# A graph layer with gathers of h held longer, lists of rows and the second dst moved between them, and one-hot rows in buffers of their own

## The chip, the cores and the metric

The kernel runs on one core of a Trainium2 chip. The metric is the time of one execution in microseconds on the device: the median of several runs. A profile of one execution shows what each engine did: PE (TensorE, products), DVE (VectorE), ACT (ScalarE), POOL (GpSimd, which here issues the indexed gathers) and SP (SyncE, which issues plain transfers).

## The reference

One message-passing layer over 6,250 nodes and 206,250 edges that are sorted by their target (`dst`).

```python
h = jnp.maximum(_layernorm(x, axis=-1), 0.0)
msg = h[src] + edge_attr_64                       # 206250 x 64
agg = jax.ops.segment_sum(msg, dst, num_segments=6250)
out = x + jax.nn.relu(agg @ W1 + b1) @ W2 + b2
```

All arrays are float32; x is 6250 x 64, W1 64 x 128 and W2 128 x 64.

## The kernel before

The sum over edges is split. The edges' own features are summed by target with one-hot products: `chunk_hot` (L380) makes one-hot rows on DVE, `chunk_sum` (L392) multiplies them with the features into the PSUM tile `bank`, ACT copies the result (`by_node`, L395) and `chunk_place` (L404) adds it to a block's PSUM tile `pv`. The part `h[src]` is not gathered for most edges. The kernel counts instead how often each source stands at each target: for lists of 128 edges, `count` makes one-hot rows of the source's low and high parts (`hot_lo`, `hot_key`, L699), multiplies them (L707, PSUM tile `pc`), ACT copies the counts to SBUF (L709), and `multiply` multiplies the counts with h (L742 and L745, into `pv`).

The last 24 groups of 1,024 edges (GA to G) go another way. `load_h` (L823) loads a group's features into a tile `pfeat` (four buffers), and POOL adds the rows of h to them with 8 indexed gathers per group from a table in memory (L252). `features_h` takes a pair of groups: `sum_groups` makes one-hot rows `hotp` (L421), multiplies them with the two tiles (L425, also into `bank`), and copies to `sum_p` (L428); `add_sums` (L414) adds that to the sums on DVE. At its end `features_h` asks for the pair two further on (`fetch_h`), whose tiles take the two buffers that have just been read.

The main loop has 310 steps: 22 blocks of targets with 14 steps each, one of them with 16. A pair of one-hot tiles is made on DVE in every even step, for two steps. Work that does not belong to the counting is hung on steps: `before` runs ahead of a step's counting, `later` behind its products. POOL's order is settled when the kernel is built: `queue` holds gathers with a planned cost each, `pool[0]` is POOL's planned time, `clock(n)` the planned time of step n (1.6 us per step for the first 14, then 1.38), and after each step POOL gets what is planned to begin up to 5 us later. A pair is multiplied in the first step for which

```python
if h_next < G and fetched.get(h_next + 1, 1e9) + LAND_US <= clock(n):
    features_h(h_next)
    h_next += GB
    add_later(n + 5)
```

where `fetched` is the planned time at which the pair's last gather was issued. What has not been multiplied by the end of the loop is multiplied behind it.

The head, before the loop, does three things. It finds where each list of edges begins: `fetch_row` gathers rows of `dst` (15 lists of 128), `seek` counts in them on ACT (L268), and `place` (L272, L274) writes `first` and `first_i` on DVE. From `first_i`, `fetch_pair` gathers the packed words of two lists, `unpack_pair` and `turn_pair` make the keys. It normalizes x: `norm_mean`, `norm_center` (which lets ACT square), `norm_var`, `norm_root`, `norm_scale`, `norm_h` (which writes the table); `norm_b` and `norm_c` split h in three bfloat16 parts within the first steps. And it finds the targets of the edge chunks: `chunk_starts`, `chunk_rows`, `chunk_columns`, `chunk_index` give `cols_i`, `fetch_dst` gathers `dstq`, `chunk_nodes` (L337, L338) and `chunk_turn` (L345) turn it into `rel`, which `chunk_hot` reads.

The order of each engine is that of the program text: a manual schedule records the operations as they are called. An engine that waits holds all that stands behind it in its queue.

Of the kernel before, what the change touches and what calls it, by code (L numbers as in the profile page):

```python
# [18 lines left out]
P = 128  # L19
N = 6250  # L20
E = 206250
D = 64
# [11 lines left out]
J = 8  # L34
# [3 lines left out]
W = 42  # L38
# [56 lines left out]


HEAD_US = 1.6
STEP_US = 1.38
GATHER_US = 2.2
WORDS_US = 2.6  # L100
LAND_US = 5.0
NEED_P = N - 31 * GP - 6


@with_exitstack
def gnn_kernel(ctx: ExitStack, tc: tile.TileContext, x, src_t, dst_t, dst_g, edge, w1, b1, w2, b2, out):
# [196 lines left out]
    def chunk_columns(t0, t1, tag="po", bufs=1):  # L303

        px = ps.tile([P, NT + 1], F32, tag=tag, name="pcols", bufs=bufs)
        n = (t1 - t0) * RC
        assert n <= JP * RC
        quarters = late.tile([P, JP * RC, JQ], F32, tag="dstq", bufs=2, name="quarters")[0:1, :n]
        nc.vector.tensor_tensor(quarters, starts[:, t0 * RC:t1 * RC].unsqueeze(2).to_broadcast([1, n, JQ]),
                                row_e.unsqueeze(1).to_broadcast([1, n, JQ]), op=OP.add)  # L310
        rows = [(t, quarters[:, (t - t0) * RC:(t - t0 + 1) * RC, :]) for t in range(t0, t1)]
        if t0 == 0:
            rows.append((NT, row_n))
        for t, of in rows:
            nc.tensor.matmul(px[:, t:t + 1], of.rearrange("o c q -> o (c q)"), ones[0:1, 0:1], start=True, stop=True)
        known["t", t0] = px
# [12 lines left out]
    def fetch_dst(t):  # L329
        dsts[t] = late.tile([P, CQ], I32, tag="dstq", bufs=2, name="dstq")  # L330
        gather(dsts[t], dst_g.rearrange("q h (k o) -> (q h k) o", o=1), cols_i[:, t:t + 1])
# [85 lines left out]
    def sum_groups(g, tiles):  # L417
        pa = bank[:, :GB * W].rearrange("p (b w) -> p b w", b=GB)
        for b in range(GB):
            hot = work.tile([P, J, W], F32, tag="hot", name="hotp")  # L420
            nc.vector.tensor_tensor(hot, rel_p[:, g - GA + b, :].unsqueeze(2).to_broadcast([P, J, W]),  # L421
                                    iota[:, :W].unsqueeze(1).to_broadcast([P, J, W]), op=OP.is_equal)
            for j in range(J):
                k = j % 2 * D
                nc.tensor.matmul(pa[k:k + D, b, :], tiles[b][:, j, :], hot[:, j, :],  # L425
                                 start=(j < 2), stop=(j >= J - 2))
        sum_p = work.tile([P, GB, W], F32, name="sum_p", bufs=1)
        nc.scalar.activation(sum_p, pa, AF.Copy)  # L428
        to_add.append((g, sum_p))
# [122 lines left out]
    nc.scalar.dma_start(packed.rearrange("(q k) o -> q (k o)", q=QA), dstn[:QA].rearrange("q h k -> q (h k)"))  # L552
    seek(0, 6)
    place(0, 3)
    norm_mean()
    place(3, 3)
    fetch_pair(0)
    for i in range(6, 11):
        fetch_row(i)
    for k in range(3):  # L560
        norm_center(k)
        seek(6 + k, 1)
    fetch_pair(2)
    for k in range(3):
        norm_var(k)
    norm_root()
# [287 lines left out]
    for g in range(GA, GA + 2):  # L854
        load_h(g)
    for i in range(11, IC):
        fetch_row(i)
    place(6, 3)
    chunk_starts(0, 2 * RC, "pc", 2)
# [5 lines left out]
    turn_pair(0)  # L865
    seek(9, 3)
    norm_scale()
    chunk_index(0, 2)
    fetch_dst(0)
    fetch_dst(1)  # L870
    for k in range(3):
# [5 lines left out]
    todo = {}  # L877

    def then(k, f):
        todo[k] = f()  # L880

    before = {
        1: [lambda: seek(12, 3), lambda: chunk_nodes(0)],
        2: [lambda: [fetch_h(g) for g in range(GA, GA + 4)], lambda: chunk_turn(0)],
        3: [lambda: place(9, 3), lambda: open_pv(0, True)],
        5: [lambda: place(12, 3)],
        7: [lambda: norm_b(0)],
        9: [lambda: norm_b(1)],
        11: [lambda: norm_b(2)],
        13: [find_groups],  # L890
        15: [lambda: norm_c(0), lambda: clear(0, 5)],
        17: [lambda: norm_c(1), lambda: clear(1, 5)],
        19: [lambda: norm_c(2), lambda: clear(2, 5)],
        21: [lambda: clear(3, 5)],
        23: [lambda: clear(4, 5)],
# [18 lines left out]
    for k in range(1, (IC + 1) // 2):  # L914
        n = 12 + 10 * k
        if k > 1:
            before.setdefault(max(n - 20, 3), []).append(lambda k=k: queue.insert(0, (WORDS_US, lambda: fetch_pair(2 * k))))
        before.setdefault(n, []).append(lambda k=k: unpack_pair(2 * k))
        before.setdefault(n + 1, []).append(lambda k=k: turn_pair(2 * k))
    for t in range(1, NT):  # L920
        n = 24 if t == 1 else 64 + 4 * t
        if t > 1:
            before.setdefault(n, []).append(lambda t=t: queue.insert(0, (GATHER_US, lambda: fetch_dst(t))))
        before.setdefault(n + 8, []).append(lambda t=t: chunk_nodes(t))
        before.setdefault(n + 9, []).append(lambda t=t: chunk_turn(t))
# [57 lines left out]
    for n, (b, s) in enumerate(steps):  # L983
# [23 lines left out]
        if n >= 3:  # L1007
            if h_next < G and fetched.get(h_next + 1, 1e9) + LAND_US <= clock(n):
                features_h(h_next)
                h_next += GB  # L1010
                add_later(n + 5)
# [152 lines left out]
```

## Time and profile before

| | |
|---|---|
| median of 9 runs | 539.95 us (538.48 to 542.29) |
| the profiled execution | 539.93 us, span 538.2 us |
| PE busy | 456.3 us (85%) |
| DVE busy | 417.1 us (77%) |
| POOL busy | 424.1 us (79%) |
| ACT busy | 353.3 us (66%) |
| main loop, first one-hot rows to last counting products | 40.5 to 513.5 us of the span |
| the 192 gathers of h | 46.3 to 508.0 us, 1.9 us each |

A line of the timeline gives start, duration, engine, line, operation, tiles and count; in brackets stands how long the engine had rested before and what it waited for. A line of the windows gives the window, its length, the busy time of PE, weight loads, DVE, ACT and POOL, the granted TensorE clock (1.00 is full), the share of the DMA engines and GB/s. In the chain, the shares say on which engine's work the end of the run hung.

### The profile page before, as it was taken

The numbers are of one execution on the slowest core, as the hardware profiler recorded it, in microseconds if no ns is written. First come the engines' busy times: TensorE is split into PE (matmuls) and PEld (weight loads), VectorE is DVE, ScalarE is ACT, GpSimd is POOL, SyncE is SP. The second block draws the span as 40 slices with busy tenths as digits, with TensorE's granted clock in tenths as the row PEclk, the third lists the DMA queues.
The fourth block names the chain that finished last, engine by engine and source line by source line (L and its number), as shares of the span: only waits on it lengthen the run. The fifth ranks groups of instructions, "written<-read, shape, count | busy, mean of one in ns | idle before, by whom it ended". The sixth has DMA issues, their size and how long they took to land.

```text
span 538.2 us, 19106 instructions
## 1 busy us (share of the span) xinstructions
PE 456.3 (85%) x8183; PEld 384.8 (71%) x8184; DVE 417.1 (77%) x618; ACT 353.3 (66%) x534; POOL 424.1 (79%) x265
## 2 busy tenths in 40 slices
PE   3015678899987999888989999999999999999994
PEld 3014566777876887667778877888888778888883
DVE  4787998778797979849789769788697597797720
ACT  4357897677574756787657765767667676677621
POOL 6676898888897878889888888888888888888600
PEclk9999899999998999999999999999999999999998
DMA  8839703555655666554575665665666666667540
GB/s 225 227 117 285 191 12 65 141 139 144 168 141 157 159 160 174 144 119 130 135 176 130 142 149 120 144 175 144 143 175 142 146 172 147 171 144 146 132 130 15
DMA packets 113544, 79.04 MB, mean 147 GB/s; under 512 B 32920, under 2 KB 108686, under 8 KB 113230
## 3 DMA queue, kind: packets, MB, share of 16 engines
q1 hardware_dynamic: 83962, 65.99, 42.1%
q0 software_dynamic: 29200, 10.25, 16.1%
q10 hardware_dynamic: 292, 1.52, 0.9%
q8 instruction: 66, 1.08, 0.8%
q14 instruction: 24, 0.20, 0.1%
HBM read 73.74 MB, written 3.99 MB: 144 GB/s over the span
## 4 chain that ended last, share of the span: by engine, by line
PE 69%; DVE 12%; ACT 6%; issue 5%; DMA 5%; POOL 2%; DVEq 0%; ACTq 0%
PE pc L707 22%; PE pv L742 16%; PE pv L745 11%; PE bank L392 10%; DVE hot_lo L699 4%; ACT counts L709 3%; DVE hot_key L699 3%; PE pv L404 3%; PE ph L798 2%; DMA dstq<-in_dst_g,cols_i 2%; PE po L805 2%; POOL rows L252 2%; DMA rows<-in_dst_g,row_i 2%; PE bank L425 2%; ACT over L666 1%
## 5 line engine op out<-in xcount | busy, mean ns | idle before, releaser
L252 POOL DMA_INDIRECT pfeat<-table,src_p x192 | 363.9, 1895 | 62.1 <-issue 53.3
L709 ACT ACTIVATE counts<-pc 128x882 bf16<-128x882 f32 x310 | 272.9, 909 | 42.9 <-PE pc L707 29.7
L707 PE MATMUL pc<-hot_key,hot_lo 128*128 128x147 bf16 x1860 | 175.1, 231 | 30.4 <-DVE hot_key L699 15.3
L699 DVE TENSOR_TENSOR hot_lo<-iota_lo,keys 128x1536 bf16<-128x1536 bf16 x155 | 147.7, 953 | 41.0 <-PE pc L707 38.7
L707 PEld LDWEIGHTS <-hot_lo 128*128 128x128 bf16 x1860 | 134.9, 100 | 59.5 <-issue 25.3
L699 DVE TENSOR_TENSOR hot_key<-iota_key,keys 128x1776 bf16<-128x1776 bf16 x155 | 166.9, 1077 | 0.0
L742 PE MATMUL pv<-counts,h 128*128 128x252 bf16 (+1 forms) x1078 | 148.7, 272 | 0.1
L742 PEld LDWEIGHTS <-h 128*128 128x128 bf16 x1078 | 99.0, 97 | 8.2 <-issue 0.2
L745 PE MATMUL pv<-counts,h 128*64 128x252 bf16 (+1 forms) x1078 | 76.0, 275 | 0.0
L395 ACT ACTIVATE by_node<-bank 128x128 f32<-128x128 f32 x66 | 18.4, 279 | 84.1 <-PE bank L392 49.0
L392 PE MATMUL bank<-feat,hot 128*21 128x64 f32 x3168 | 66.5, 222 | 6.4 <-issue 3.8
L392 PEld LDWEIGHTS bank<-feat,hot 128*21 128x21 f32 x3168 | 49.4, 101 | 21.5 <-issue 17.5
L745 PEld LDWEIGHTS <-h 128*64 128x64 bf16 x1078 | 54.2, 111 | 3.6 <-issue 0.4
L380 DVE TENSOR_TENSOR hot<-rel,iota 128x504 f32<-128x504 bf16 x66 | 44.6, 677 | 8.8 <-PE bank L425 8.4
L252 POOL DMA_INDIRECT words<-packed,first_i x15 | 25.8, 1720 | 8.0 <-DMA packed<-dstn 3.7
L421 DVE TENSOR_TENSOR hotp<-dst_p,iota 128x336 f32<-128x336 f32 x24 | 11.9, 506 | 25.1 <-PE bank L392 18.5
L252 POOL DMA_INDIRECT rows<-in_dst_g,row_i x15 | 17.0, 1132 | 6.7 <-issue 3.4
L404 PE MATMUL pv<-select,by_node 128*64 128x42 f32 x264 | 21.4, 244 | 0.7 <-ACT by_node L395 0.7
L404 PEld LDWEIGHTS pv<-select,by_node 128*64 128x64 f32 x264 | 13.4, 137 | 9.4 <-issue 1.1
L294 PE MATMUL pstart<-begins,first 128*1 128x9 f32 (+2 forms) x30 | 1.3, 172 | 19.8 <-DVE first L272 19.4
L798 PE MATMUL ph<-sums,w1s 128*128 128x252 f32 (+1 forms) x50 | 15.5, 391 | 1.5 <-DVE sums L414 0.9
L754 DVE TENSOR_TENSOR sums<-sums,pv 128x252 f32<-128x252 f32 x22 | 9.0, 409 | 8.6 <-PE pv L745 8.6
(171 smaller groups left out, 274.7 us busy)
## 6 DMA issues: line engine op xcount, KB each, us to landing
feat<-in_edge SPq DMA_DIRECT2D x132, 384.0 KB
pfeat<-in_edge SPq DMA_DIRECT2D x24, 256.0 KB
pfeat<-table,src_p POOLq DMA_INDIRECT x192
out_y<-y SPq DMA_DIRECT2D x24, 63.0 KB
xs<-in_x SPq DMA_DIRECT2D x4, 315.0 KB
dstn<-in_dst_g SPq DMA_DIRECT2D x1, 1024.0 KB
table<-xl SPq DMA_DIRECT2D x2, 512.0 KB
packed<-dstn ACTq DMA_DIRECT2D x1, 768.0 KB
```

The lines of the kernel that those rows point to most:

```text
L252: nc.gpsimd.indirect_dma_start(out=rows, out_offset=None, in_=source, in_offset=bass.IndirectOffsetOnAxis(ap=index, axis=0), compute_op=op)
L380: nc.vector.tensor_tensor(hot_of[u][:, :n].rearrange("p c j w -> p (c j) w"), rel[:, c:c + n].rearrange("p c q k -> p (c q k)").unsqueeze( ...
L392: nc.tensor.matmul(bank[q * QP:q * QP + WQ, i * D:(i + 1) * D], hot[:, i, j, :], feat[i][:, j, :], start=(k == 0), stop=(k == JP - 1))
L395: nc.scalar.activation(by_node[u][:, :n].rearrange("p c d -> p (c d)"), bank[:, :n * D], AF.Copy)
L404: nc.tensor.matmul(pvs[b][0][i * D:(i + 1) * D, a:a + CN], of[:, i, :], select, start=False, stop=False)
L421: nc.vector.tensor_tensor(hot, rel_p[:, g - GA + b, :].unsqueeze(2).to_broadcast([P, J, W]), iota[:, :W].unsqueeze(1).to_broadcast([P, J, ...
L699: nc.vector.tensor_tensor(hot.rearrange("p t (m o) -> p t m o", o=2), iota_k.rearrange("p (m o) -> p m o", o=2).unsqueeze(1).to_broadcast( ...
L707: nc.tensor.matmul(pc[:, k, m * K:(m + 1) * K], hot_lo[:, j, :], hot_key[:, j, :K], start=True, stop=True)
L709: nc.scalar.activation(counts[b % 2][:, :, s * ST * V:(s + 1) * ST * V].rearrange("p h (k m) -> p h k m", k=2), pc[:, :, :ST // 2 * K].rea ...
L742: nc.tensor.matmul(pv, h3[:, h, :2 * D], of, start=(h == 0 and not clear), stop=False)
L745: nc.tensor.matmul(pv[k:k + D, :], h3[:, h, 2 * D:], of, start=False, stop=(h >= HI - 2))
L798: nc.tensor.matmul(ph[:, :n], w1s, agg[:, start[b]:start[b + 1]], start=True, stop=True)
```

## The change

- `sum_groups` makes its one-hot rows in blocks of four columns of edges (128 x 168) in a tag `hotp` of its own with two buffers, four blocks per pair of groups. Before, a block held eight columns (128 x 336) and shared the two buffers of the tag `hot` with `chunk_hot`.
- The tiles `quarters` and `dstq` share one buffer instead of two.
- A pair of groups is multiplied once its last gather was planned 22 us ago (`HELD_US`), no longer 5 (`LAND_US`).
- In the head, seven lists' rows are fetched instead of fifteen; `norm_mean` comes ahead of the first `place`, and the squares come ahead of the `seek` of lists 3 to 6. Rows 7 to 10 and 11 to 14 are put at the front of POOL's queue at steps 3 and 14, and their `seek` and `place` go to steps 12 to 14 and 20 to 22.
- The third pair of word gathers is issued in the head, behind the first dst. The dst gathers of 1 to 4 are queued at step 24 and at 74, 84, 94 (before: in the head, and at 72, 76, 80); each is used 8 steps later as before.

```diff
+HELD_US = 22.0
...
-        quarters = late.tile([P, JP * RC, JQ], F32, tag="dstq", bufs=2, name="quarters")[0:1, :n]
+        quarters = late.tile([P, JP * RC, JQ], F32, tag="dstq", name="quarters")[0:1, :n]
...
-        dsts[t] = late.tile([P, CQ], I32, tag="dstq", bufs=2, name="dstq")
+        dsts[t] = late.tile([P, CQ], I32, tag="dstq", name="dstq")
...
         for b in range(GB):
-            hot = work.tile([P, J, W], F32, tag="hot", name="hotp")
-            nc.vector.tensor_tensor(hot, rel_p[:, g - GA + b, :].unsqueeze(2).to_broadcast([P, J, W]),
-                                    iota[:, :W].unsqueeze(1).to_broadcast([P, J, W]), op=OP.is_equal)
             for j in range(J):
-                k = j % 2 * D
-                nc.tensor.matmul(pa[k:k + D, b, :], tiles[b][:, j, :], hot[:, j, :],
-                                 start=(j < 2), stop=(j >= J - 2))
+                k = j % 4
+                if k == 0:
+                    hot = work.tile([P, 4, W], F32, name="hotp")
+                    nc.vector.tensor_tensor(hot, rel_p[:, g - GA + b, j:j + 4].unsqueeze(2).to_broadcast([P, 4, W]),
+                                            iota[:, :W].unsqueeze(1).to_broadcast([P, 4, W]), op=OP.is_equal)
+                h = slice(j % 2 * D, (j % 2 + 1) * D)
+                nc.tensor.matmul(pa[h, b, :], tiles[b][:, j, :], hot[:, k, :], start=(j < 2), stop=(j >= J - 2))
...
-    seek(0, 6)
+    seek(0, 3)
+    fetch_row(6)
+    norm_mean()
     place(0, 3)
-    norm_mean()
-    place(3, 3)
     fetch_pair(0)
-    for i in range(6, 11):
-        fetch_row(i)
     for k in range(3):
         norm_center(k)
-        seek(6 + k, 1)
+        if k < 2:
+            seek(3 + 2 * k, 2)
+    norm_var(0)
+    norm_var(1)
+    place(3, 4)
     fetch_pair(2)
-    for k in range(3):
-        norm_var(k)
+    norm_var(2)
     norm_root()
...
-    for i in range(11, IC):
-        fetch_row(i)
-    place(6, 3)
...
-    seek(9, 3)
     norm_scale()
     chunk_index(0, 2)
     fetch_dst(0)
-    fetch_dst(1)
+    fetch_pair(4)
...
+    def rows_later(a, z):
+        queue[:0] = [(1.25, lambda i=i: fetch_row(i)) for i in range(a, z)]
...
-        1: [lambda: seek(12, 3), lambda: chunk_nodes(0)],
+        1: [lambda: chunk_nodes(0)],
...
-        3: [lambda: place(9, 3), lambda: open_pv(0, True)],
-        5: [lambda: place(12, 3)],
+        3: [lambda: open_pv(0, True), lambda: rows_later(7, 11)],
+        12: [lambda: seek(7, 2)],
+        13: [lambda: seek(9, 2), find_groups],
+        14: [lambda: place(7, 4), lambda: rows_later(11, IC)],
...
+        20: [lambda: seek(11, 2)],
+        21: [lambda: clear(3, 5), lambda: seek(13, 2)],
+        22: [lambda: place(11, 4)],
...
-        if k > 1:
-            before.setdefault(max(n - 20, 3), []).append(lambda k=k: queue.insert(0, (WORDS_US, lambda: fetch_pair(2 * k))))
+        if k > 2:
+            before.setdefault(n - 20, []).append(lambda k=k: queue.insert(0, (WORDS_US, lambda: fetch_pair(2 * k))))
...
-        n = 24 if t == 1 else 64 + 4 * t
-        if t > 1:
+        n = 24 if t == 1 else 54 + 10 * t
+        if t > 0:
             before.setdefault(n, []).append(lambda t=t: queue.insert(0, (GATHER_US, lambda: fetch_dst(t))))
...
-            if h_next < G and fetched.get(h_next + 1, 1e9) + LAND_US <= clock(n):
+            if h_next < G and fetched.get(h_next + 1, 1e9) + HELD_US <= clock(n):
```

More of the change, by code (lines that the diff above doesn't have):

```diff
@@ L889, in gnn_kernel @@
         11: [lambda: norm_b(2)],
-        13: [find_groups],
         15: [lambda: norm_c(0), lambda: clear(0, 5)],
@@ L893, in gnn_kernel @@
         19: [lambda: norm_c(2), lambda: clear(2, 5)],
-        21: [lambda: clear(3, 5)],
+        20: [lambda: seek(11, 2)],
+        21: [lambda: clear(3, 5), lambda: seek(13, 2)],
+        22: [lambda: place(11, 4)],
         23: [lambda: clear(4, 5)],
```

## The prediction

> **What bounds the kernel now.** I read the page's busy shares and chain first, then the rests of each engine, then the timeline at the head, at a group of gathers late in the loop, and at the end.
>
> ```profile
> PE 456.3 (85%) x8183; PEld 384.8 (71%) x8184; DVE 417.1 (77%) x618; ACT 353.3 (66%) x534; POOL 424.1 (79%) x265
> PE 69%; DVE 12%; ACT 6%; issue 5%; DMA 5%; POOL 2%; DVEq 0%; ACTq 0%
> L252 POOL DMA_INDIRECT pfeat<-table,src_p x192 | 363.9, 1895 | 62.1 <-issue 53.3
> ```
>
> PE carries the chain, so after the head the loop runs at PE's pace. POOL's 79% hides a second bound: the 192 gathers of h follow one another without a pause from 46 us on (363.9 us busy, 53.3 us of issue gaps), and nothing in the chain shows it because POOL is done at 508 us while the last of its groups is read at 524 us. The end of the loop shows how near that is:
>
> ```profile
> 466.37 1.13 PE L425 MATMUL bank<-hotp,pfeat 128*64 128x42 f32 x32
> 467.10 1.78 SPq L823 DMA_DIRECT2D pfeat<-in_edge  x2
> 472.14 2.06 POOL L252 DMA_INDIRECT pfeat<-table,src_p  x1 [1.14 <-PE bank L392]
> 502.63 1.55 POOL L252 DMA_INDIRECT pfeat<-table,src_p  x1 [0.30 <-issue]
> 504.48 1.65 POOL L252 DMA_INDIRECT pfeat<-table,src_p  x1 [0.30 <-issue]
> 506.44 1.56 POOL L252 DMA_INDIRECT pfeat<-table,src_p  x1 [0.30 <-issue]
> 494.25 0.96 PE L707 MATMUL pc<-hot_key,hot_lo 128*128 128x147 bf16 x12
> 523.94 1.13 PE L425 MATMUL bank<-hotp,pfeat 128*64 128x42 f32 x32
> ```
>
> The tenth pair of groups is multiplied at 466.37; that frees two pfeat buffers, SP loads the last pair's edge rows into them, and POOL, which had to wait 1.14 us, starts the last 16 gathers 5.8 us after the products began. The last one starts at 506.44. So the place of the tenth pair in the loop fixes when the last gather can land.
>
> The head, and a long gather in it:
>
> ```profile
> 18.56 3.42 DVE L449 TENSOR_REDUCE stat<-xl 128x49 f32<-128x3136 f32 x1
> 32.26 0.19 DVE L465 TENSOR_SCALAR stat<-stat 128x49 f32<-128x49 f32 x1
> 36.82 0.16 DVE L320 CAST cols_i<-pcols 128x2 int32<-128x2 f32 x1 [0.26 <-PE pcols L315]
> 39.37 2.03 POOL L252 DMA_INDIRECT dstq<-in_dst_g,cols_i  x1 [0.31 <-issue]
> 45.35 0.42 DVE L337 TENSOR_SCALAR dstq<-dstq,cols 128x384 f32<-128x384 int32 x1 [2.91 <-DMA dstq<-in_dst_g,cols_i]
> 65.26 10.83 POOL L252 DMA_INDIRECT words<-packed,first_i  x1 [0.30 <-issue]
> 166.43 0.42 DVE L337 TENSOR_SCALAR dstq<-dstq,cols 128x384 f32<-128x384 int32 x1 [3.35 <-DMA dstq<-in_dst_g,cols_i]
> 170.00:173.00 3.00, 3.00 (x24) 2.48 (x24) 2.90 (x6) 2.04 (x3) 1.14 (x1) 0.50 0.14 16
> ```
>
> DVE sums x, the variance is scaled at 32.26, the columns for dst are known at 36.82, but POOL issues dst 0 only at 39.37, behind lists of rows; DVE stands 2.91 us for it. Again at 166.43 DVE stands 3.35 us for dst 2; PE then rests 2.59 us, and the last line shows the granted clock at 0.50 for the three microseconds behind that rest.
>
> **The head: -5.8 us.** The mean moves ahead of the first lists and ACT's squares ahead of seeks 3 to 6. DVE is free from 15.6; x has landed by 18.56 at the latest. With the rows' durations (mean 3.42 + 0.34, centre 1.14, square 1.06, two seeks 1.2, variance 1.2) the scaling falls at 28.1 if the mean starts at 15.6 and at 30.6 if it starts at 18.56; I take the middle, 29.3, 3.0 earlier than now. The chain to cols_i loses 0.27 us of list arithmetic: 33.55. On POOL, seven rows and four word gathers are over by 27.3 (each 0.95 + 0.3, packed landing at 21.4 as now), so dst 0 is issued at once and used 5.98 us later, as now: 39.5 instead of 45.35. The gain is 5.8 us (4.5 to 7.0 from the two ends). The second dst, two words and the rows' lists queue behind dst 0 while POOL waits for the table anyhow (3.03 us of rest now), so they cost nothing there; without that cover they cost 4 x 1.25 us. The table, and gathers of h with it, come 3.0 us earlier; four rows and dst 1 in between (6.5 us) take that back, less a word pair moved ahead (2.6): POOL gains nothing. DVE is busy without a gap from 53 to 76 us, so the 5.8 us survive to step 22.
>
> **The held groups: the end.** HELD_US makes a pair wait 22 us of planned time instead of 5. Placing the pairs by the planner's rule, products stand after steps 33, 65, 97, 123, 149, 174, 200, 225, 251, 276, 302 and once after the loop before; after the change at 55, 86, 116, 143, 168, 194, 219, 245, 270, 296 and twice after the loop. The tenth pair, which lets the last 16 gathers begin, is now at step 296. That step's PE work ends at 494.7 in the trace. With G the time saved by then, the sum is:
> - start of the tenth pair's products: 494.7 - G
> - to the first of the last 16 gathers: +5.8 (466.37 to 472.14)
> - 15 intervals: 13 us of loop remain, 6 intervals at 2.29 (472.14 to 506.44), then 9 at 1.9 (last two rows, DVE mostly idle): +30.8; the last one's own 1.6
> - landing: the 16th gather ended at 95.64 and its products ended at 98.44 without a rest, so at most 2.6; a dst gather landed 4.5 after its end. I take 2.5 (0 to 4.5)
> - last product 0.1 and the unchanged end: 538.2 - 525.1 = +13.1
> - PE's clock: it would reach these products at 523.9 - G and stand some 10 us; after 2.59 us of rest it got 0.50 for about 3.5 us, so half of that is lost: +1.7 (0 to 1.7)
>
> That is a span of 550.3 - G, and with 1.7 us around the span (539.93 - 538.2) a time of 552.0 - G. The profiled 539.93 equals the median 539.95. The change gains only if G passes 12.
>
> **G after the head.** dst gathers move to 54 + 10t, use eight steps later. Before dst 2, POOL now has 37 gathers of h instead of 40, nine words instead of eleven, but four rows and dst 1 more: 2.9 us less, and it starts 3.0 earlier, so it is issued near 155 and lands near 160.5; step 82 wants it near 165.8 - 5.8 = 160. The rest of 2.59 us and the slow clock behind it (half of 3.5) go but for a little: -3.5 (0 to -4.3). The tile is single now, so the next dst gather waits for the transposes of the last; those come one step after its use and the gathers 12 us apart, so I cost that at nothing; if late, it holds POOL for 2.1 us, as one did at 171.9.
>
> One-hot rows: DVE makes four blocks of 168 instead of two of 336. A block is between 0.25 (half of 506 ns) and 0.51; 0.30 by the 128x252 rows at 0.41: 0.2 us more DVE per pair, hidden where DVE leads. Two waits go: "hotp <- PE bank L392" 18.5 us over 7 and "hot <- PE bank L425" 8.4 over 4. One comes: the third block takes the first one's buffer, so DVE stands until PE has done the first four products of this very pair. Behind it DVE has block four, then hot_lo and hot_key of the next two steps, for which PE waits. If the pair ends an odd step, PE has nothing else: 0.2 + 2 x 0.30 + 0.87 + 1.0 = 2.7, less the 0.85 left of the pair's products: 1.8 us. If it ends an even step, one step of work covers it but for 0.4. Before step 296 four are odd (55, 143, 219, 245) and five even: 9.2 us. Rests of PE around products now, from PE's timeline: 0.46, 0.97, 0.43, 0.43, 0.91, 0.49, 0.43, 0.91, in sum 5.0; and one pair fewer stands before step 296 (1.13). Net +3.1; the ends are -6 (all rests go, nothing comes) and +8.
>
> G = 5.8 + 3.5 - 3.1 = 6.2, so 545.8 us.
>
> **A rule weighed.** Rows 11 to 14 are now gathered near 62 to 67, and ACT wants them at steps 20 and 21, near 69, with DVE and PE behind. In that stretch one gather took 10.83 us now, with DVE running two-input instructions without a gap from 65 to 75, while the three gathers ahead of it (59.70 to 64.95) took 1.55 beside the same kind of instruction. One in ten gathers between 46 and 76 was caught, so I leave it out of the sum and price it as a rival. The Trainium skill, "SBUF — State Buffer", section "Who interferes with whom", says that a DVE instruction with two SBUF inputs contends with a GpSimd instruction that reads SBUF; if the gather's index counts as such a read, all four rows would be held until DVE itself stops, and the estimate would be 553; the short gathers speak against so strict a reading.
>
> **The rivals.**
> - Lockout: the long gather of 65.26 falls on the lists of rows. DVE goes gap-free to about 69, rows follow to 74, land by 79, and DVE, waiting in place, loses about 7.5 us: 553. For it: the 10.83. Against it: nine in ten gathers passed.
> - Faster, by DVE's freedom: the 26.9 us of DVE rests on products go and take PE's rests on hot_key with them (15.3 us in the list of waits), because DVE stands in the third block only where it has a lead. It decides once G passes 13.7. With the head at 7.0, dst at 4.3 and +6 from the buffers, G is 17.3 and the time 535. Against it: the wait in the third block is certain in the order of DVE.
> - No difference: G between 10.4 and 13.7; or G between 5.8 and 9.1 with all gathers 1.86 apart and no slow clock (2.9 and 1.7 us less), so that the end eats the head's gain almost exactly: 540. Against the second: 2.29 beside a working DVE.
> - That holding the pairs does nothing, because gathers lie off the path: then 552.0 is replaced by 539.9 and the time is 534. It falls with the 1.14 us rest of POOL at 472.14: POOL already follows the products.
>
> **How the numbers follow.** Slower by the late last gathers, 541.6 to 549.5: 0.57. Lockout or worse, above that: 0.14. Faster (both ways): 0.14. Within 0.3% (1.6 us, about what a measurement here can tell from no change): 0.15. The range 538.5 to 551 leaves out most of the faster case and the upper half of the lockout.
>
> **What would show it.** Right: dst 0 used near 39.5; the tenth pair's products near 488; POOL resting before the last 16 gathers and the last starting near 525; PE resting some 10 us on pfeat near 518 to 529, then a granted clock of 0.50. Wrong: POOL done before PE leaves the loop; PE's rests on hot_key after products gone; a row gather of 5 us or more near 65.

## The result and the profile after

The changed kernel takes 560.12 us (median of 20 runs, 554.75 to 563.6) against 540.25 for the kernel before in the same comparison (62 runs): a ratio of 1.0358, 95% interval 1.0336 to 1.0379. The forecast was 545.8 with a range up to 551. The sign was right, the size was missed by 14 us. The profiled execution has a span of 558.1 us. Two of the 20 runs, and below two of the four of c_hotp4_held5 and one of the four of a_hotp4_held5, are more than 1.5% above the fastest of their kernel; no difference is read from these alone.

The rows of its page that correspond to those shown of the kernel before, the busy shares and the gathers of h:

```profile
PE 470.1 (84%) x8183; PEld 393.5 (71%) x8184; DVE 418.8 (75%) x640; ACT 356.0 (64%) x534; POOL 411.0 (74%) x265
L254 POOL DMA_INDIRECT pfeat<-table,src_p x192 | 359.7, 1873 | 88.0 <-issue 53.0
```

Of its timeline, the tenth pair with the last 16 gathers, the head, and dst 2 (start, duration, what; the rest before it in brackets):

```profile
503.32 0.67 PE L429 MATMUL bank<-hotp,pfeat 128*64 128x42 f32 x16
504.05 1.34 SPq L827 DMA_DIRECT2D pfeat<-in_edge  x2
508.14 2.00 POOL L254 DMA_INDIRECT pfeat<-table,src_p  x1 [5.36 <-PE pc L711]
538.35 1.54 POOL L254 DMA_INDIRECT pfeat<-table,src_p  x1 [0.30 <-issue]
542.09 0.44 PE L429 MATMUL bank<-hotp,pfeat 128*64 128x42 f32 x2 [1.49 <-DMA pfeat<-table,src_p]
...
28.49 0.19 DVE L468 TENSOR_SCALAR stat<-stat 128x49 f32<-128x49 f32 x1
32.75 0.16 DVE L322 CAST cols_i<-pcols 128x2 int32<-128x2 f32 x1 [0.27 <-PE pcols L317]
38.93 0.44 DVE L339 TENSOR_SCALAR dstq<-dstq,cols 128x384 f32<-128x384 int32 x1 [0.56 <-DMA dstq<-in_dst_g,cols_i]
169.33 0.41 DVE L339 TENSOR_SCALAR dstq<-dstq,cols 128x384 f32<-128x384 int32 x1
```

The head and the end came as forecast. dst 0 is used at 38.93 (forecast 39.5), dst 2 without a rest. From the tenth pair's products at 503.32 to the end of the span it is 54.8 us (forecast 55.6). What failed lies between. The products should have begun at 488.5, six us earlier than the work of that step before; they began at 503.32. The list of waits shows where to look (total in us, number of waits, longest). First the kernel before, then the changed one:

```profile
DVE hotp L421 <- PE bank L392: 18.5, 7, 5.4
PE pc L707 <- DVE hot_key L699: 15.3, 16, 2.6
POOL pfeat L252 <- PE pc L707: 2.7, 9, 0.3
```

```profile
DVE hotp L426 <- PE bank L429: 41.4, 17, 6.1
PE pc L711 <- DVE hot_key L703: 27.2, 15, 5.6
POOL pfeat L254 <- PE pc L711: 27.1, 8, 7.1
```

DVE stands 41.4 us ahead of one-hot rows, where it stood 18.5 before; PE's rests on hot_key rose from 15.3 to 27.2; and POOL, which hardly waited for PE in its line of gathers before (2.7), waits 27.1.

To see where time goes I took the start of ACT's eviction of the counts (L713) at each of the 310 steps and set it against the kernel before. The head's lead is 6.8 us at step 12. By step 32 it has become a loss of 2.2. Between steps 55 and 60, at the first pair of groups, another 4.7 us are lost, of which 1.1 are the pair's own products. Between steps 75 and 85, where dst 2 fell, 3.5 us come back. The loop then wavers between a lead of 0.6 and a loss of 3.6 up to step 180, loses 4 us at each of the pairs of steps 219 and 245, and ends at a loss of 9.3 (step 309: 522.8 against 513.5). The pair at step 55 shows the new wait in the timeline:

```profile
127.42 0.57 DVE L426 TENSOR_TENSOR hotp<-dst_p,iota 128x168 f32<-128x168 f32 x2
133.09 0.58 DVE L426 TENSOR_TENSOR hotp<-dst_p,iota 128x168 f32<-128x168 f32 x2 [5.10 <-PE bank L429]
133.59 0.96 DVE L703 TENSOR_TENSOR hot_lo<-iota_lo,keys 128x1536 bf16<-128x1536 bf16 x1
134.47 1.08 DVE L703 TENSOR_TENSOR hot_key<-iota_key,keys 128x1776 bf16<-128x1776 bf16 x1
...
132.05 0.62 PE L429 MATMUL bank<-hotp,pfeat 128*64 128x42 f32 x16
133.48 0.68 PE L429 MATMUL bank<-hotp,pfeat 128*64 128x42 f32 x16 [0.81 <-DVE hotp L426]
135.60 1.66 PE L711 MATMUL pc<-hot_key,hot_lo 128*128 128x147 bf16 x12 [1.45 <-DVE hot_key L703]
```

And the windows of the same stretch (time, length, then busy time of each engine, granted clock, DMA share, GB/s):

```profile
134.00:137.00 3.00, 1.55 (x18) 1.43 (x15) 3.00 (x4) 0.68 (x2) 0.00 (x0) 0.75 0.70 191
137.00:140.00 3.00, 3.00 (x26) 2.49 (x23) 2.98 (x5) 2.07 (x3) 2.67 (x2) 0.68 0.14 16
```

DVE makes two half blocks at 127.42 and is then some four us ahead of PE. The third needs the first one's buffer, so DVE stands 5.10 us until PE gets there, and arrives with no lead at all: PE waits 0.81 in the pair and 1.45 behind it, and its granted clock (third number from the end) falls to 0.75 and 0.68. The forecast had priced the bubble, the work that PE must wait for (1.8 us for pairs in odd steps, 0.4 for even ones). Step 55 is odd; the bubble here is 2.3, a slow clock comes on top, and DVE has its lead to earn again. The clock is the smaller part: of the ten pairs in the loop three are followed by 3.41 us at a clock of 0.50 (from 135.5, 388.1 and 429.0), which loses at most 1.7 us each.

### The profile page after: what moved, and what is told of

It reads as the page before. It is cut to its first block, busy times and chain, and to the rows that moved or that the text cites. A ratio compares the mean times of both kernels' runs of the same rounds, so it can differ in the third digit from the quotient of the medians.

```text
span 558.1 us, 19160 instructions
## 1 busy us (share of the span) xinstructions
PE 470.1 (84%) x8183; PEld 393.5 (71%) x8184; DVE 418.8 (75%) x640; ACT 356.0 (64%) x534; POOL 411.0 (74%) x265
## 3 DMA queue, kind: packets, MB, share of 16 engines
q0 software_dynamic: 29200, 10.25, 15.6%
## 5 line engine op out<-in xcount | busy, mean ns | idle before, releaser
L254 POOL DMA_INDIRECT pfeat<-table,src_p x192 | 359.7, 1873 | 88.0 <-issue 53.0
L713 ACT ACTIVATE counts<-pc 128x882 bf16<-128x882 f32 x310 | 275.3, 907 | 57.5 <-PE pc L711 41.7
L711 PE MATMUL pc<-hot_key,hot_lo 128*128 128x147 bf16 x1860 | 178.8, 234 | 34.7 <-DVE hot_key L703 27.2
L711 PEld LDWEIGHTS <-hot_lo 128*128 128x128 bf16 x1860 | 137.4, 101 | 63.5 <-DVE hot_key L703 35.0
L746 PE MATMUL pv<-counts,h 128*128 128x252 bf16 (+1 forms) x1078 | 152.7, 276 | 0.1
L426 DVE TENSOR_TENSOR hotp<-dst_p,iota 128x168 f32<-128x168 f32 x48 | 14.5, 330 | 44.1 <-PE bank L429 41.4
L254 POOL DMA_INDIRECT words<-packed,first_i x15 | 19.8, 1320 | 7.1 <-issue 3.7
L254 POOL DMA_INDIRECT dstq<-in_dst_g,cols_i x5 | 6.4, 1278 | 24.7 <-PE pdst L347 12.8
L429 PE MATMUL bank<-hotp,pfeat 128*64 128x42 f32 x384 | 17.9, 235 | 7.0 <-DVE hotp L426 3.5
L429 PEld LDWEIGHTS bank<-hotp,pfeat 128*64 128x64 f32 x384 | 14.2, 137 | 11.1 <-DVE hotp L426 5.4
```

Of the source, the lines that this page charges most:

```text
L254: nc.gpsimd.indirect_dma_start(out=rows, out_offset=None, in_=source, in_offset=bass.IndirectOffsetOnAxis(ap=index, axis=0), compute_op=op)
L426: nc.vector.tensor_tensor(hot, rel_p[:, g - GA + b, j:j + 4].unsqueeze(2).to_broadcast([P, 4, W]), iota[:, :W].unsqueeze(1).to_broadcast([ ...
L429: nc.tensor.matmul(pa[h, b, :], tiles[b][:, j, :], hot[:, k, :], start=(j < 2), stop=(j >= J - 2))
L711: nc.tensor.matmul(pc[:, k, m * K:(m + 1) * K], hot_lo[:, j, :], hot_key[:, j, :K], start=True, stop=True)
L713: nc.scalar.activation(counts[b % 2][:, :, s * ST * V:(s + 1) * ST * V].rearrange("p h (k m) -> p h k m", k=2), pc[:, :, :ST // 2 * K].rea ...
L746: nc.tensor.matmul(pv, h3[:, h, :2 * D], of, start=(h == 0 and not clear), stop=False)
```

## The experiments

The runs were made in five lots. The chips differ, so each run is read against the kernel before on its own chip; a clear case of that is in the section on the hardware. Names that begin with b are the kernel before with one edit, the others the changed kernel, most of them with edits. "Line" is the start of the last gather of h, "309" the start of ACT's eviction at the last step, all in us of the profiled run. The kernel before was traced only for the main comparison.

| kernel | time | before there | ratio, 95% | 309 | line | span |
|---|---|---|---|---|---|---|
| before | | | | 513.5 | 506.4 | 538.2 |
| changed | 560.12 | 540.25 | 1.0336 to 1.0379 | 522.8 | 538.4 | 558.1 |
| a_held5 | 554.38 | 543.08 | 1.0144 to 1.0276 | 526.0 | 522.8 | 553.3 |
| a_place | 558.36 | 543.08 | 1.0223 to 1.0376 | 522.1 | 537.6 | 557.1 |
| a_hotp4 | 540.19 | 543.08 | 0.9931 to 1.0008 | 502.7 | 518.4 | 537.5 |
| a_hotold | 544.45 | 543.08 | 1.0008 to 1.0085 | 506.8 | 522.3 | 542.0 |
| a_hotp4_held5 | 530.62 | 523.75 | 1.0104 to 1.0217 | 484.9 | 503.8 | 522.8 |
| a_hotown | 526.24 | 523.75 | 1.0022 to 1.0092 | 481.2 | 506.1 | 525.8 |
| a_all | 533.25 | 523.75 | 1.0070 to 1.0245 | 486.7 | 511.1 | 530.9 |
| b_held22 | 521.13 | 523.75 | 0.9929 to 0.9980 | 492.0 | 502.2 | 519.6 |
| c_after | 536.82 | 523.45 | 1.0229 to 1.0319 | 499.4 | 515.2 | 534.2 |
| c_hotp4 | 527.90 | 523.45 | 1.0012 to 1.0124 | 481.3 | 506.4 | 525.1 |
| c_hotp4_held5 | 527.48 | 523.45 | 1.0040 to 1.0186 | 484.0 | 501.1 | 519.8 |
| c_short | 512.81 | 523.45 | 0.9764 to 0.9842 | 485.8 | 481.3 | 512.6 |
| d_dst2 | 548.83 | 539.88 | 1.0059 to 1.0202 | 517.1 | 529.3 | 546.7 |
| e_hotp4_held5 | 533.16 | 524.18 | 1.0146 to 1.0219 | 486.1 | 511.2 | 530.4 |
| e_p3 | 525.97 | 524.18 | 1.0003 to 1.0050 | 498.3 | 502.9 | 525.5 |
| e_p3dst2 | 526.21 | 524.18 | 1.0023 to 1.0065 | 497.3 | 501.9 | 524.1 |

**First lot: which part of the change costs what.** The two small buffers doubled (and one buffer for rows of lists less, for room):

```
-                    hot = work.tile([P, 4, W], F32, name="hotp")
+                    hot = work.tile([P, 4, W], F32, name="hotp", bufs=4)
```

> The changed kernel with four buffers for the one-hot blocks of a pair instead of two (rows of lists in five buffers instead of six, for the space), so that no block waits for products of its own pair. Theory (DVE stands 41.4 us in 17 waits for the pair's first products, and PE then waits for the next hot_lo and hot_key): that rest falls below 5 us and the time by 8 to 10 us, to 551 us. Rival (DVE has the time, so its rest costs PE nothing): within 2 us of the changed kernel.

The old way of making them put back (whole blocks, in the buffers shared with the list groups):

```
+            hot = work.tile([P, J, W], F32, tag="hot", name="hotp")
```

> The changed kernel with one-hot rows of the pairs as before: two blocks of 336 in the two buffers shared with the chunks. Theory (the new buffers cost about 8 us net, since the shared ones wait for products further back): 552 us. Rival (the shared buffers wait as much, 27 us of DVE rest before): within 2 us of the changed kernel.

Hold back at 5 us (`HELD_US = 5.0`):

> The changed kernel with pairs held for 5 us of planned time again, all else as changed. Theory (the end waits for the last 16 gathers, which start only behind the tenth pair's products at 503.3 us): the tenth pair comes some 20 steps earlier, the last gather lands before PE reaches the last pair, and the 10.7 us that the end lost between the last step (+9.2 us against before) and the span's end (+19.9 us) come back: 549 us. Rival (the hold is what keeps PE from waiting for gathers inside the loop): PE rests on pfeat appear inside the loop and eat it, 556 to 562 us.

Lists 7 to 14 turned into keys later:

```
-        14: [lambda: place(7, 4), lambda: rows_later(11, IC)],
+        20: [lambda: place(7, 4)],
-        22: [lambda: place(11, 4)],
+        38: [lambda: place(11, 4)],
```

> The changed kernel with the second and third part of the lists read and written later: place of lists 7 to 10 at step 20 instead of 14, seek of lists 11 to 14 at steps 30 and 31 instead of 20 and 21, their place at step 38 instead of 22. Theory (DVE runs ahead of ACT and POOL, and the two places make it stand 2.33 and 4.63 us for sums whose rows land late; between steps 12 and 26 the lead over before falls from 7.0 to -2.5 us): both rests vanish, the lead at step 26 is 5 to 7 us, and the time falls by about 9 us to 551 us, since the end follows the tenth pair. Rival (DVE and POOL are in each other's way there and the rest only moves to the next words or to dst 1): below 3 us.

Four buffers take away more than the theory gave them: step 309 falls by 20.1 us, the time to 0.997 of the kernel before. The old shared blocks do nearly as much, 16.0 us at step 309. The list of waits with four buffers:

```profile
DVE hotp L426 <- PE bank L429: 5.7, 3, 4.9
PE pc L711 <- DVE hot_key L703: 19.5, 9, 5.5
```

The same pair of groups in its timeline:

```profile
126.02 1.05 DVE L426 TENSOR_TENSOR hotp<-dst_p,iota 128x168 f32<-128x168 f32 x4
127.01 0.96 DVE L703 TENSOR_TENSOR hot_lo<-iota_lo,keys 128x1536 bf16<-128x1536 bf16 x1
```

All four half blocks are made without a stop and DVE goes on to the next step. Taking the hold back gave about 4 us beside a_place on the same chip, and some 8 by the ratios of the changed kernel and of a_held5 to the kernel before (1.0358 and 1.0210): between theory and rival. The last gather started 15.6 us earlier, but the loop then set the end (553.3 is 27.3 behind step 309). The later lists kept the head's lead to step 24 and lost it by step 30 to other rests, PE's on ACT's copies of the counts and a clock of 0.50 from 83.4 on; at step 309 they are worth 0.7 us, and in time their interval overlaps that of the changed kernel.

**Second lot: what stands behind it.**

> The changed kernel with one-hot rows of a gathered group made in one whole block as before the change, but in two buffers of their own of that size (so both blocks of a pair have a buffer, and none is shared with the list groups' rows). Theory (what costs is that the pair's third half block finds no free buffer, and what helps is a buffer for everything that a pair makes): as fast as four half buffers, 537 to 542 us, with hardly any rest of the vector engine ahead of these rows. Rival (the halves themselves are what makes it slow or fast, the ownership is nothing): 543 to 547, as with the shared buffers.

```
+            hot = work.tile([P, J, W], F32, tag="hotp", name="hotp", bufs=2)
```

> The changed kernel with four small buffers for the one-hot rows of gathered groups (one per half block of a pair) and the hold of the last pairs back at 5 us. Theory: two costs, each its own. The wait for the third half block is gone (worth about 20 us alone), and with the loop that fast the end is set by the last 16 gathers, which the hold of 22 us starts late; with 5 us they start earlier and the end comes about 24.5 us after step 309, as before the change: step 309 near 503, span 528 to 532, time 529 to 534. Rival: the hold protects the loop, gathers that start earlier make the loop's own gathers late, and the time stays at 537 to 542, that of the four buffers alone.

> Four small buffers, the hold at 5 us, and the lists 7 to 14 turned into keys some six steps later than in the change. Theory: four buffers and the hold give 529 to 534 as in the run beside this, and the lists, no longer made when their rows have not landed, keep 3 to 6 us more of the lead of the head: 524 to 530. Rival: the lead is lost to another wait at steps 20 to 30 whatever the lists do, and the time is within 2 us of the run without the later lists.

> The kernel before the change with only its hold of gathered pairs set from 5 to 22 us. Theory: the hold delays the last pairs' gathers whatever else was changed, and the last gathers set the end: slower by 6 to 12 us, 546 to 553, with the matrix engine at rest ahead of the last pair. Rival: in the old loop the last gathers have slack enough, or the earlier gathers cost the loop as much as the hold costs the end: within 3 us of the kernel before.

The kernel before took 523.75 us on this chip, so the absolute times expected mean nothing and the ratios and traces are read. Two whole blocks of their own run the loop as well as four halves (481.2 against 484.9 at step 309, though the hold differs): the halves are not what costs, room for all that a pair makes is. The loops of a_hotp4_held5 and a_hotown end 18 and 21 us ahead of a_hotp4's, most or all of it by the chip, on which the kernel before too is 19 us faster. The span does not follow in full: it ends 38 and 45 us behind step 309, and 19.0 and 19.6 behind the start of the last gather. That suggests that the line of gathers had become the end. The later lists brought nothing (a_all within the spread of a_hotp4_held5). And the hold alone, on the old kernel, did not cost the 6 to 12 us of my theory: its ratio is 0.9954, and it is the only version whose whole interval lies below that of the kernel before. Why is open, since the kernel before was not traced on this chip.

**Third lot: is the line of gathers the second bound?** The changed kernel and its four-buffer forms on one chip, and the last pair's gathers left out:

```
-        for j in range(J):
+        for j in range(J if g < G - 2 else 0):
```

> The changed kernel itself, beside the three runs below on one chip, since the chips differ (the kernel before took 543.1 us on the chip of the first four experiments and 523.8 us on that of the second four). Theory (the third half block stops the vector engine, the held pairs then set the end): the loss does not hang on the chip, 1.02 to 1.045 of the kernel before. Rival (the loss comes from the slower matrix engine of the first chip, and where the loop is fast the gathers alone set the end): on a fast chip below 1.015.

> The changed kernel with four small buffers, the hold left at 22 us. Theory: 0.99 to 1.00 of the kernel before on a chip like the first (0.9969 there), and on a chip like the second near the 1.0057 of the two whole buffers. In both cases 15 us or more below the changed kernel beside it. Rival: less than 8 us below it.

> Four small buffers and the hold back at 5 us. Theory (gathers of h are a second bound of their own: some 1.9 us and 0.3 us for each, in one line from 46 us on, then 19 us from the last one's start to the end; the hold costs only where that line has slack): on a chip like the first, where the loop is slow, the line of gathers ends near 506 us and the loop's end near 527 is no longer waited for: 525 to 531, faster than before the change by 2 to 3%. On a chip like the second the line already ran without a rest, so within 4 us of the run with 22 us. Rival: the hold is worth nothing on either chip: within 3 us of the run with 22 us.

> Four small buffers, hold at 5 us, and the 16 gathers of h for the last pair left out (its products take the edge rows alone, so that part of the sum is missing). Theory (the line of gathers sets the end): the last gather starts some 30 us earlier, the loop's end takes over, 24.5 us behind step 309: 509 to 516 on a chip like the second, 526 to 531 on one like the first (where it then gains little over the run with all gathers). Rival (the end belongs to the matrix engine's loop): within 3 us of the run with all gathers on either chip.

The loss does not hang on the chip (1.027). Four buffers move step 309 by 18.1 us, as in the first lot by 20.1, but the time by only 8.9, less than the 15 of the theory. The hold makes no difference that can be told: 522.1 to 528.4 us with it, 521.5 and 524.9 in the two faster executions without. Without the last 16 gathers all four executions take 512.5 to 514.3 us, some 10 less than those two: the line does set the end. The end of the line in the timeline of c_hotp4:

```profile
504.55 1.54 POOL L254 DMA_INDIRECT pfeat<-table,src_p  x1 [0.30 <-issue]
506.39 1.54 POOL L254 DMA_INDIRECT pfeat<-table,src_p  x1 [0.30 <-issue]
```

and the last gather in that of c_short:

```profile
481.25 2.39 POOL L254 DMA_INDIRECT pfeat<-table,src_p  x1 [0.30 <-issue]
```

From 380 us on the line of c_hotp4 runs with nothing but the 0.30 us of issue between gathers, and the span (525.1) ends 18.7 us behind the last start. In c_short it ends 31.3 us behind it, as in the kernel before (31.8), and 26.8 behind step 309. So the runs fit two bounds, up to some 3 us: 24.7 to 27.3 us behind step 309, or 17.3 to 19.8 behind the start of the last gather, whichever is later. Where the two nearly meet the run does not tell which it was: e_p3 and e_p3dst2 end 27 behind the one and 22 behind the other, b_held22 27.6 and 17.5.

On this chip the cost of the third block's wait can be read pair by pair, since c_after and c_hotp4 multiply their pairs in the same steps. From a pair's step to the next the difference between their evictions grows by 1.9 to 2.3 us at each of the four odd pairs and by 0.2 to 0.5 at each of the five even ones, 10.1 in all; the forecast had 9.2. But between steps 50 and 292, over the same nine pairs, it grows by 16.1: another 6 us come in the steps behind the pairs.

**Fourth and fifth lot: what slows the line.** Two dst buffers again (`tag="dstq", bufs=2`), first with three buffers for rows of lists, then cleanly beside a run with three small one-hot buffers:

> Four small buffers, hold at 5 us, and two buffers for the second lists' columns (dst) again, as before the change (the rows of lists then have three buffers). Theory (with the third half block's wait gone, the line of gathers sets the end, and the single dst buffer stops that line for 2 to 9 us): the last gather 5 to 9 us earlier, 520 to 524 on a chip like the second, 0.99 to 1.00 of the kernel before. Rival (those rests of the gather line are made good later, it has slack): within 2 us of the run with the single buffer, 1.01 of the kernel before there.

> Three small buffers for the one-hot rows, hold at 5 us, one dst buffer, four buffers for rows of lists. Theory: the third half block finds a buffer and only the fourth waits, for the first half's products of its pair; by then the vector engine has less of the pair ahead of it but still stands in its place, so about half of what four buffers gave over two is lost: 4 to 9 us above the run with four on a chip where the kernel before takes 540, 0 to 5 where it takes 524. Rival (any third buffer is enough): within 2 us of the run with four.

> The run with three small buffers, with two dst buffers instead of one and nothing else changed: the clean form of a run in which the rows of lists ran short of buffers. Theory (the single dst buffer stops the line of gathers for 2 to 9 us in one or two places, and that line is one of the two bounds): 3 to 7 us faster than with one dst buffer where the line sets the end, within 2 us where the loop does. Rival (the line makes such a stop good): within 2 us on either chip.

> Four small buffers and the hold at 5 us once more, beside the two runs below. Theory (two bounds: the loop's end 24.5 us behind step 309, and the last gather's start plus 19 us): on a chip where the kernel before takes near 540 us, where its loop is the higher bound, 0.965 to 0.985 of it, since both bounds fall; where the kernel before takes near 524, 1.00 to 1.02, as twice before. Rival (the hold is worth nothing with fast buffers): 0.99 to 1.00 on the first kind of chip.

d_dst2 tells nothing of dst: with three buffers POOL waited 21.0 us for rows of lists to be read and the line of h began at 59.8 instead of 45.5. The clean pair differs by 0.2 us: the stop on dst (10.8 us in e_p3) went, and a stop of 13.3 on second_n took its place; and here the loop may have set the end (27 us behind step 309). So the single dst buffer is not shown to cost anything; where the line is the bound it was not tried cleanly.

Two further runs gathered 22 groups instead of 24 (`GP = 22`), in the form of d_dst2 and in the kernel before:

> The same as the run with two dst buffers, and 22 of the groups gathered instead of 24: one pair moves to the lists, so there are 16 gathers fewer and one unit and some more list work for the matrix and vector engines; all is computed. Theory (two bounds, gather line and loop, and here the line is the higher): the line ends some 30 us earlier and the loop sets the end, 3 to 8 us later than its own end in the run with the last pair left out: 515 to 521 on a chip like the second, 0.98 to 0.995 of the kernel before. Rival (the list work costs the loop more than the line gives back): 524 or more.

> The kernel before the change with 22 groups gathered instead of 24. Theory: the kernel before is bound by its loop (its last gather starts 31.8 us ahead of the end, where the kernels bound by gathers show 17 to 20), so fewer gathers give nothing and the added list work costs 3 to 8 us: 1.00 to 1.015 of the kernel before. Rival: gathers bound it too, and it gains as much as the changed kernel's variant does.

They say nothing of the question: both took 4550 us, nearly all of it in code that the other runs never enter (L1116 to L1127, 1616 gathers of hsrc). By the code that is the way for lists that do not fit.

e_hotp4_held5 landed on a fast chip again, so its forecast for the other kind stays untested. But it shows where the same kernel loses 10.6 us between two profiled executions, on two chips on which the kernel before differs by 0.7 (521.5 in c_hotp4_held5, 532.2 here). Its loop runs nearly as in c_hotp4_held5 (486.1 against 484.0 at step 309); its line ends 10 us later (511.2 against 501.1), with seven gathers of 4 to 5.5 us instead of three. One of them, with DVE around it, from the timeline of e_hotp4_held5:

```profile
197.22 4.86 POOL L254 DMA_INDIRECT pfeat<-table,src_p  x1 [0.30 <-issue]
202.38 1.54 POOL L254 DMA_INDIRECT pfeat<-table,src_p  x1 [0.30 <-issue]
...
196.41 1.06 DVE L426 TENSOR_TENSOR hotp<-dst_p,iota 128x168 f32<-128x168 f32 x4
197.38 0.68 DVE L382 TENSOR_TENSOR hot<-rel,iota 128x504 f32<-128x504 bf16 x1
197.98 0.82 DVE L792 TENSOR_TENSOR xs<-xs,b2s 126x640 f32<-126x640 f32 x1
198.71 0.95 DVE L703 TENSOR_TENSOR hot_lo<-iota_lo,keys 128x1536 bf16<-128x1536 bf16 x1
199.58 1.08 DVE L703 TENSOR_TENSOR hot_key<-iota_key,keys 128x1776 bf16<-128x1776 bf16 x1
```

Over the whole run: of 30 gathers of h in whose first 1.55 us DVE was busy for less than half, none took over 2.3 us (mean 1.57); of 126 with DVE busy for 90% or more, 18 did (mean 2.08). So long gathers stand beside a busy DVE. That is not the whole cause: c_hotp4_held5 has 125 gathers beside so busy a DVE, and only 9 of them took over 2.3 us; its three longest stand at the same places as three of the seven here (near 142, 232 and 374 us). What picks them is open.

In e_p3 DVE stands for the fourth half block:

```profile
DVE hotp L426 <- PE bank L429: 34.6, 12, 5.3
```

Its loop is 12.2 us later than that of e_hotp4_held5 on the same chip, and yet it is 7 us faster in time, against both theories for it. Its gathers of h take 359.5 us in all against 376.6. A DVE that stands may be the reason; this is not shown, since the four buffers of c_hotp4_held5 came to 360.7 without such stops.

## Why the prediction was right or wrong

The sum was 552.0 - G, where G is the time saved by the tenth pair's products (494.7 less their start). The step that failed is G, and in it first the price of the one-hot rows.

- **The sum around G, right.** Four versions that hold their pairs on the slower chips test it, though they were run for something else (the kernel before takes 540.25 us beside the changed one and 543.08 beside the others). In us:

| kernel | tenth pair | G | 552.0 - G | measured |
|---|---|---|---|---|
| changed | 503.32 | -8.6 | 560.6 | 560.12 |
| a_place | 502.46 | -7.8 | 559.8 | 558.36 |
| a_hotold | 488.26 | 6.4 | 545.6 | 544.45 |
| a_hotp4 | 483.10 | 11.6 | 540.4 | 540.19 |

  On the fast chips c_after and b_held22 end 53.7 and 55.2 us behind the start of their tenth pair, where the forecast had 55.6. c_hotp4 and a_hotown end 62 us behind it: there POOL was still busy with earlier gathers when the tenth pair was multiplied (the last 16 began 15 us behind it), so the tenth pair no longer set the end.

- **Head, right.** The forecast was -5.8; the lead is 6.8 us at step 12, and the scaling falls at 28.49 instead of the 29.3 assumed. (The forecast's terms for the scaling, as printed, do not show how they add up to 28.1 and 30.6.)
- **dst, right.** The forecast was -3.5, and 3.5 us came back between steps 75 and 85. The single tile, priced at nothing or 2.1 for POOL, stopped POOL for 12.8 us in two places; no run shows that this cost time.
- **One-hot rows, the step that failed.** A net loss of 3.1 us was forecast (9.2 for the new wait, less 5.0 of old rests and 1.1 for the pair that moves), with 8 as the bad end. Against the old shared blocks the loop lost 16.0 us (506.8 to 522.8), against four buffers 20.1 (18.1 on the chip of the third lot). The mechanism was named, and its place in DVE's order. The size was wrong because the price was the bubble alone (the half blocks and the next hot_lo and hot_key, less what PE still had to do). The bubbles came nearly as priced, 10.1 us for 9.2. What the price left out is what comes behind them: DVE stands from where it arrives until PE arrives, up to 5.4 us in the loop, so it gives up its lead at each pair, even steps too, and the list work that follows has no lead to hide behind. That this lost lead is the rest of the loss is read from the traces and not tested by itself. The slow clock after a rest is a small part. The half blocks themselves took 330 ns instead of 300, which is 1.4 us in all.
- **Lists of rows, priced at nothing: wrong.** DVE stood 2.33 and 4.63 us for ACT's inrow, PE then 3.59 and 5.63 for hot_key, and ran at a clock of 0.50 near 62 and 79. The timeline of the changed kernel:

```profile
59.25 0.17 DVE L274 SCALAR_TENSOR_TENSOR first<-first,middle 128x4 f32<-128x4 f32 x1 [2.33 <-ACT inrow L270]
61.53 1.66 PE L711 MATMUL pc<-hot_key,hot_lo 128*128 128x147 bf16 x12 [3.59 <-DVE hot_key L703]
75.17 0.17 DVE L274 SCALAR_TENSOR_TENSOR first<-first,middle 128x4 f32<-128x4 f32 x1 [4.63 <-ACT inrow L270]
78.36 0.92 PE L711 MATMUL pc<-hot_key,hot_lo 128*128 128x147 bf16 x6 [5.63 <-DVE hot_key L703]
```

  The lead fell by 9.0 us between steps 12 and 32. Not all of that is the lists': in a_place, without these two rests, it fell by 6.4. The forecast named ACT, DVE and PE behind the four rows, but put a cost there only for a gather that is locked out. It was not that: the rows of 64.33 to 71.4 took 1.0 to 1.9 us each.
- **G in all.** The forecast was 6.2, and -8.6 was measured. With the old blocks, a_hotold, it is 6.4, where the forecast without the terms of the blocks (5.8 + 3.5, and 1.1 for the pair that moves) would be 10.4: so some 4 us of the miss lie in the lists and elsewhere in the loop, and the rest in the blocks. That 6.4 is near the forecast 6.2 is luck.
- **The end, right in sum, with one wait wrong.** From the tenth pair to the end it is 54.8 us, forecast 55.6; the pair stands at the step forecast, and POOL rests 5.36 us ahead of the last 16 gathers. The clock of 0.50 lasted 6.8 us instead of 3.5. But PE was to stand some 10 us for the last gathers and stood 1.49:

```profile
536.44 0.67 PE L429 MATMUL bank<-hotp,pfeat 128*64 128x42 f32 x16
538.96 0.67 PE L429 MATMUL bank<-hotp,pfeat 128*64 128x42 f32 x16 [0.37 <-ACT sum_p L431]
```

  The last pair's products were to be reached at 523.9 - G, which is 532.5 with the G measured; PE began them at 538.96, in part because a second pair now stands after the loop ahead of them (536.44). So the last gather and PE arrived nearly together: the path by the gathers came out as added up, the wait of PE did not.
- **"Gains only if G passes 12", not general.** It fits the chip of the profile, where a_hotp4 with G at 11.6 came out even. But the hold is not 12 us lost whatever else goes on: in the changed kernel its removal gave 4 to 8, with four buffers on a fast chip nothing that can be told, and in the old kernel on a fast chip adding it cost nothing. There the rival that holding does nothing came near.
- **The faster rival** had it that freeing DVE decides. Four buffers do free it, and on the chip of the first lot that about evened the time, but no version with the whole change is clear of the noise below the kernel before. On the fast chips the line of gathers is next.
- **The rule weighed.** The Trainium skill, "SBUF — State Buffer", section "Who interferes with whom", says that a DVE instruction with two SBUF inputs contends with a GpSimd instruction that reads SBUF. I left it out of the sum. The count of long gathers beside a busy DVE agrees with it in kind, not in the strict reading: 108 of those 126 gathers stayed below 2.3 us.

## What to carry to other kernels

Count the tiles that a producer makes in a round before its consumer is done with the first. With fewer buffers than that the producer stops once per round, and the price can be more than the bubble at that place: here 16 us where the bubbles were 10, because the producer's lead goes too. Write the end as the later of two lines (here loop and gathers) and work out both after the change; what frees one may slow the other. On chips that differ by 3% compare only kernels that ran on the same one.

## What the hardware showed that was not expected

- The kernel before took 539.9 and 543.1 us on two chips (540.25 in the main comparison) and 523.5 to 524.2 on three others. In the traces, the 3168 chunk products are 65.5 to 67.7 us of PE's time on the slow chips and 57.4 to 58.8 on the fast ones, at the same mean of 220 to 223 ns for one; the cause is open.
- Gathers of h lengthen beside a DVE without gaps, up to 9.1 us from 1.55 (a_place and a_all, at 58 us). How many do changes between profiled executions of the same kernel: three over 4 us in a_hotp4_held5 and c_hotp4_held5, seven in e_hotp4_held5. Three stand at the same places in all of them.
- The clock stood at 0.50 for 6.8 us around and after the rests of 3.59, 5.63 and 1.49 us, and for 3.4 us after the rest of 2.59 in the kernel before, so its length does not follow the rest. In all 18 traces (those of 4550 us apart) every stretch at 0.50 that ends inside the run is 3.41 us long or a whole multiple of it, up to 11. The Trainium skill, "TensorE: Matmul & The Clock Gate", section "Part 1: The HAM clock gate", tells of free-running windows of about 3.4 us, which agrees; why it was one window here and two there is not shown.
- In the changed kernel the clock is 0.50 from 16.0 to 46.8 us, through the head and the first steps, and in the kernel before it is full there. The head's lead came all the same.
